# Two graph-attention layers with a mixture of experts: one pair a step and shared weight fetches in the tail, and the second layer's weights prepared later

## The chip, the cores and the metric

The kernel runs on one core of a Trainium2 chip. A core has five engines that run side by side, each with its own queue of instructions that it takes in order: PE (TensorE, matrix products), DVE (VectorE, elementwise work, sums and 32x32 transposes), ACT (ScalarE, functions of one argument), POOL (GpSimd, here small elementwise work and the indirect transfers) and SP (SyncE, which only issues transfers). PEld is the loading of PE's stationary operand. The metric is the time of one execution on the device, in microseconds. Before the change the median of three runs was 1665.73 us (1664.08 to 1666.54).

## The reference

The input x is 64 batches of 256 rows of 256 float32 numbers, with one 256 x 256 adjacency matrix for all batches. With LN for the layer norm, the reference does

```
x = x + elu(heads(softmax(mask(leaky_relu(e_src + e_dst))) @ q))   q = LN(x) @ W0, 4 heads of 64
x = x + LN(x) @ Wf.T + bf
x = x + relu(softmax(mask(leaky_relu(e_src + e_dst))) @ h)         h = LN(x) @ W1, one head
t = LN(x)
logits = t @ router.T ; the two largest of 8, weights renormalised to sum 1
x = x + t + sum over the two experts of weight * (gelu(t @ w1[e] + b1[e]) @ w2[e] + b2[e])
```

where e_src and e_dst are the products of q (or h) with the two halves of a vector a. The last layer is a mixture of 8 experts of which each row uses two.

## The kernel before

**The work.** A batch of 256 rows is two tiles of 128 rows. `batch_layers` carries a batch through both attention layers, the linear layer between them and the router's logits, in 20 pieces. Piece by piece it yields, so that the pieces of several batches interleave. The weights of an attention layer are widened by columns that yield e_src and e_dst directly: `score_columns` multiplies the weights with both halves of a (DVE, line 197), sums (200), scales, and subtracts the column mean (`center`, 158), which spares the norm's mean later. `prepare_f` transposes and centers the weights of the linear layer; `fill_mask` turns the adjacency into a mask, on PE through a transpose.

**The experts.** The first 62 batches are *routed*: 12 chunks of 4 batches, 6 of 2 and 2 of 1 (`CHUNKS`). When a chunk's logits are there, `route` places each row, twice, in a region of DRAM for its expert (`send`, line 877, an indirect transfer on POOL). As regions fill, `expert_pair` takes 256 rows of one expert (a *pair* of tiles): four transfers of 64 KB bring them into xr, one brings the row numbers and weights (xt), one brings the expert's 288 KB of first-layer weights (`we`, from the packed copy `wpack`). DVE turns the rows (sT, line 116), PE makes ph (`hidden`, 783), ACT applies gelu, PE makes py with the resident second-layer weights (`result`, 798), DVE adds b2 (y, 804), ACT scales by the row weights (776). Then `scatter` adds the 256 rows to the output with two indirect adding transfers on POOL (815). Each pair's adds wait until the adds of the pair before have landed (`added[-2:]`), because two pairs may hold the same row. The last pieces are 14 *flush* pairs, which hold what is left in the regions. There are 131 pairs in all.

The last two batches are *dense*: `dense_expert(b, e)` runs all 8 experts on all 256 rows of a batch and adds them to `base` with weights that are zero for the experts not chosen, so it needs no sends and no adds to DRAM.

**What sets the order.** From line 1041 the order of instructions is written out by hand, in *steps*. `active` holds the running generators, each with a rank; in a step every one advances by one yield, lowest rank first; a negative rank goes on within the step. A step number divided by 3 gives a phase. A batch begins every three steps (phase 2), the first in step 2, the last in step 191. `setup` jobs begin one a step from step 3 (`SETUP_AT`): prepare_f, prepare1 (the second attention layer's `score_columns`), the second mask, prepare_r, then `pack_expert` for each expert (which loads an expert's weights and writes the packed copy). In phase 1 pairs begin: two a time while batches are still to come, then three. In phase 2 up to two dense jobs begin. One scatter is issued a step. What the steps fix is the order in each engine's queue; an engine waits only where an operand, or a free buffer, is missing. `WBUFS`, `XBUFS` and `YBUFS` are the numbers of buffers for we, xr and y. `later` holds a routing job until a phase that it names.

Work issued ahead of line 1041 (constants, the first mask, the first layer's weights) is placed by the planner of the framework.

Of the kernel before, what the change touches and what calls it, by code (L numbers as in the profile page):

```python
# [9 lines left out]
F32 = mybir.dt.float32  # L10
# [17 lines left out]
def kernel(  # L28
# [108 lines left out]

    adj_i = work.tile([P, NT, N], adj.dtype, tag="z", name="adj_i", bufs=6)
    nc.scalar.dma_start(out=adj_i, in_=adj.rearrange("(t p) j -> p t j", p=P))

# [4 lines left out]
    def fill_mask(layer, op):  # L145
        mf = work.tile([P, NT, N], F32, tag="xT", name=f"maskf{layer}", bufs=4)
        nc.vector.tensor_scalar(mf, adj_i, 0.0, None, op0=op)
        pm = bank("pm", [NT, N])
        for t in range(NT):
            for j in range(NT):  # L150
                nc.tensor.transpose(
                    pm[:, j, t * P : (t + 1) * P], mf[:, t, j * P : (j + 1) * P], ident
                )
        nc.vector.tensor_copy(masks[layer], pm)

    fill_mask(0, ALU.is_gt)

# [9 lines left out]
    def gnn_weights(w, a, heads, slope, name):  # L167

        rows = lambda w, k: (
            w.rearrange("(p k) o -> k p o", k=KT) if heads > 1
            else w.rearrange("(k p) o -> k p o", k=KT)
        )[k]
        d = D // heads
        wx = const.tile([P, KT, heads, d + 3], F32, tag=name, name=name)  # L180
        for k in range(KT):
            nc.sync.dma_start(
                out=wx[:, k, :, :d],
                in_=rows(w, k).rearrange("p (h d) -> p h d", h=heads),
            )
        av = work.tile([P, 2, d], F32, tag="e", name=name + "_a", bufs=1)
        nc.scalar.dma_start(out=av.rearrange("p s d -> p (s d)"), in_=rows_to_all(a, 2 * d))
        flat = wx.rearrange("p k h c -> p k (h c)")
        return flat, lambda: score_columns(wx, av, heads, slope, name)

    def score_columns(wx, av, heads, slope, name):
        d = D // heads
        flat = wx.rearrange("p k h c -> p k (h c)")
        prod = work.tile([P, heads, d], F32, tag="hp", name=name + "_p", bufs=1)
        for k in range(KT):
            for s, c in ((0, d + 1), (1, d)):
                nc.vector.tensor_mul(
                    prod, wx[:, k, :, :d], av[:, s : s + 1, :].to_broadcast([P, heads, d])
                )
                nc.vector.tensor_reduce(wx[:, k, :, c : c + 1], prod, AX.X, ALU.add)  # L200
            nc.vector.tensor_scalar(
                wx[:, k, :, d + 1 : d + 2], wx[:, k, :, d + 1 : d + 2], 1.0 - slope, None,
                op0=ALU.mult,
            )
            nc.vector.tensor_scalar(
                wx[:, k, :, d + 2 : d + 3], wx[:, k, :, d : d + 1], slope - 1.0, None,
# [3 lines left out]

    wx0, prepare0 = gnn_weights(w0, a0, H, SLOPE0, "wx0")
    xblk = {0: load_blocks(0)}
    xin = {0: load_batch(0)}
    prepare0()
    wx1, prepare1 = gnn_weights(w1g, a1g, 1, SLOPE1, "wx1")

# [8 lines left out]
    def prepare_f():  # L225
        pw = bank("pw", [KT, D])
        for t in range(KT):
            for k in range(KT):
                nc.tensor.transpose(
                    pw[:, k, t * P : (t + 1) * P], wf_in[:, t, k * P : (k + 1) * P], ident  # L230
                )
        nc.vector.tensor_copy(wfT, pw)
        center(wfT, D)

        nc.vector.tensor_scalar(bias_f, bias_f, -1.0, None, op0=ALU.add)

    r_in = work.tile([E, D], F32, tag="x1b", name="r_in", bufs=1)
    nc.scalar.dma_start(out=r_in, in_=router)
# [10 lines left out]
    C_B1, WROW = KT * D, KT * D + 64  # L249
    WBUFS, XBUFS, YBUFS = 7, 5, 7  # L250
    wpack = tc.dram_tile([E, P, WROW], F32, name="wpack")
# [47 lines left out]
    def once(work):  # L299
# [6 lines left out]
        lambda work=work: once(work)  # L306
        for work in (prepare_f, prepare1, lambda: fill_mask(1, ALU.not_equal), prepare_r)
    ]
# [103 lines left out]
    def projected1(xT, rstd, b):  # L412
# [12 lines left out]
        for t, pq in enumerate(pqs):  # L425
# [3 lines left out]
            )  # L429
        me = work.tile([P, NT, N], F32, tag="me", name="me")  # L430
        for j in range(NT):
# [278 lines left out]
    def expert_pair(j, n, ids, ef, regs, needs):  # L710
# [23 lines left out]

        xt = small.tile([P, 2, ROW - D], F32, tag="xt", name="xt", bufs=12)
        loads.append(
# [17 lines left out]
        )  # L754
        yield 95
        xT = turned(work.tile([P, KT, PAIR], F32, tag="sT", name="sT", bufs=3), xr)
        w = small.tile([P, 2], F32, tag="w", name="w", bufs=8)
        yield 30
# [34 lines left out]

    def result(hT, e):
        py = bank("py", [2, D])
        for t in range(2):
            for f in range(KT):
# [3 lines left out]
                    start=(f == 0), stop=(f == KT - 1),  # L801
                )
        y = io.tile([P, 2, D], F32, tag="y", name="y", bufs=YBUFS)
        nc.vector.tensor_add(y, py, b2s[:, e, :].to_broadcast([P, 2, D]))  # L804
# [25 lines left out]

    def dense_expert(b, e):

        own = dense_batch[b]
        yield 90
        we = io.tile([P, WROW], F32, tag="we", name="we", bufs=WBUFS)
        nc.sync.dma_start(out=we, in_=wpack[e])
        yield 40
        yield 30
        hT = hidden(own["xT"], we)
        yield 80  # L840
        y = result(hT, slice(e, e + 1))
        for t in range(NT):
            nc.vector.scalar_tensor_tensor(
                own["base"][:, t, :], y[:, t, :], own["w"][:, t, e : e + 1],
                own["base"][:, t, :], op0=ALU.mult, op1=ALU.add,
            )
        if e == E - 1:
            while b == B - 1 and (scatters or len(added) < 2 * PAIRS):
                yield 99
            d = nc.sync.dma_start(  # L850
                out=out_rows[b * N : (b + 1) * N, :].rearrange("(t p) d -> p t d", p=P),
                in_=own["base"],
            )
            before = added[-2:] + based if b == B - 1 else []
            tc.declare_no_dep(
                d.ins, query=SYNC, group="out", keep=before,
                reason="no row is added to here, or every add is in their chain",
            )
            for ins in before:
                tc.add_manual_dep(d.ins, ins.name, AFTER, reason="filling rows were added here")  # L860
            tc.add_to_no_dep_group("out", d.ins)
            nc.sync.nop()

# [24 lines left out]
    def later(rank, *phases):  # L888

        yield rank  # L890
        while order_steps[-1] % TICKS not in phases:
            yield rank
# [103 lines left out]
    def route_dense(b, lg):  # L996
# [13 lines left out]
        dense_batch[b]["w"] = w  # L1010
        dense_jobs.extend(lambda e=e: dense_expert(b, e) for e in range(E))

# [3 lines left out]
    def jobs():  # L1016
        b = done = taken = 0
        for c, nb in enumerate(CHUNKS + (1,) * DENSE):
            nt = nb * NT
            lg = keep.tile([P, nt, E], F32, tag="lg", name=f"lg_{c}", bufs=10)  # L1020
            xng = []
# [17 lines left out]
    step, more, credit = 2, True, 0.0  # L1039
    SETUP_AT = 3  # L1040
    with tc.manual_schedule():
        while more or active or waiting or dense_jobs or scatters:
# [6 lines left out]
            if step >= SETUP_AT and setup:  # L1049
                begin(setup.pop(0)(), 90)  # L1050
            if phase == 1:
                credit = min(credit + (2.0 if more else 3.0), 3.0)
                while waiting and credit >= 1.0:
                    credit -= 1.0
                    begin(waiting.pop(0)(), 90)
            if phase == 2:
                for _ in range(2):
                    if dense_jobs:
                        begin(dense_jobs.pop(0)(), 90)
            if scatters:  # L1060
# [53 lines left out]
```

## Time and profile before

| what | value |
|---|---|
| median of the runs | 1665.73 us |
| the profiled execution's own time | 1670.08 us |
| its span, first to last instruction | 1668.3 us |
| busy: PE, DVE, ACT, POOL | 1495.5, 1317.4, 833.2, 889.4 us |
| mean granted PE clock | 0.958 |
| bytes moved | 209.74 MB, mean 126 GB/s |
| we fetches | 147 of 288 KB |
| indirect adds (line 815) | 262, 416.7 us of POOL |
| indirect sends (line 877) | 248, 251.1 us of POOL |

The span is what the engines show; the execution's own time has a little around it. Busy time is an average over stages that differ, so the stages have to be looked at one by one. A line such as "x started; idle 3.31 <- DMA out_dram" says that the engine stood idle for 3.31 us before this instruction, and that the last thing to arrive was that transfer. A transfer's issue on an engine's queue is not its duration: it lands later.

### The profile page before, as it was taken

Reading aid. Unit: us, or ns where it says so; the run is one execution under the profiler, and the core shown is the slowest. Engines: PE = TensorE matmul, PEld = TensorE weight load, DVE = VectorE, ACT = ScalarE, POOL = GpSimd, SP = SyncE. Lnnn points to the kernel's source line nnn. Section 1 sums busy time; section 2 is a strip of 40 time slices with the busy share of each in tenths; the row PEclk is TensorE's granted clock in tenths of the full one; section 3 lists DMA queues with packets and bytes.
Section 4 is the critical chain, followed back from the end, with each engine's and each line's share of the span. In section 5 each row is a group of like instructions: output and inputs, shape, how many; then the busy total and the mean of one; then the engine's idle time right before and its main releaser. Section 6 shows DMA issues by size and latency. Waiting matters only on the chain.

```text
span 1668.3 us, 30242 instructions
## 1 busy us (share of the span) xinstructions
PE 1495.5 (90%) x8474; PEld 1311.2 (79%) x8474; DVE 1317.4 (79%) x4478; ACT 833.2 (50%) x1832; POOL 889.4 (53%) x853
## 2 busy tenths in 40 slices
PE   5898888899999999999999999999989987678782
PEld 4777777688888888888888888888878876567671
DVE  6888989999898988898989898998889876423330
ACT  0243444455656666666666665655555565323221
POOL 0121433545757575757575757574764666444344
PEclk8999999999999999999999999999999998879986
DMA  3812223255757575756575766665564676866753
GB/s 107 231 41 58 61 70 94 74 142 114 167 118 163 118 159 129 140 132 146 133 149 134 145 133 146 137 140 121 123 142 99 115 156 141 200 135 112 155 107 44
DMA packets 365285, 209.74 MB, mean 126 GB/s; under 512 B 264376, under 2 KB 335040, under 8 KB 365120
## 3 DMA queue, kind: packets, MB, share of 16 engines
q1 hardware_dynamic: 314496, 139.43, 34.0%
q0 software_dynamic: 49632, 67.39, 22.5%
q8 instruction: 70, 1.15, 0.3%
q10 hardware_dynamic: 992, 0.99, 0.2%
q14 instruction: 95, 0.78, 0.2%
HBM read 118.55 MB, written 89.15 MB: 124 GB/s over the span
## 4 chain that ended last, share of the span: by engine, by line
PE 55%; DVE 26%; DMA 6%; issue 5%; POOL 4%; ACT 2%; SPq 1%; DVEq 0%; POOLq 0%; ACTq 0%
PE ph L783 14%; PE pv L475 12%; PE py L798 9%; PE pq L384 5%; PE pq L419 4%; DVE z L461 4%; PE pf L529 4%; DVE stats L353 4%; DMA out_dram<-y,xt 3%; PE pt L368 3%; POOL out_dram L815 2%; DVE mv L354 2%; PE pl L599 2%; PE pd L454 1%; DVE x L535 1%
## 5 line engine op out<-in xcount | busy, mean ns | idle before, releaser
L815 POOL DMA_INDIRECT out_dram<-y,xt x262 | 416.7, 1591 | 255.4 <-DMA out_dram<-y,xt 73.0
L475 PE MATMUL pv<-q,z 128*128 128x65 f32 (+1 forms) x2560 | 369.8, 299 | 6.7 <-DVE z L461 5.3
L475 PEld LDWEIGHTS pv<-q,z 128*128 128x128 f32 x2560 | 331.9, 194 | 19.5 <-DVE z L461 5.8
L783 PE MATMUL ph<-sT,we 128*128 128x256 f32 x1048 | 259.1, 405 | 56.2 <-DVE sT L116 47.1
L361 POOL TENSOR_SCALAR rstd<-mv 128x4 f32<-128x4 f32 (+1 forms) x132 | 69.7, 528 | 436.1 <-DVE mv L354 352.9
L877 POOL DMA_INDIRECT xs<-xng,pos x248 | 251.1, 1012 | 69.2 <-issue 66.9
L783 PEld LDWEIGHTS ph<-sT,we 128*128 128x128 f32 x1048 | 209.8, 205 | 90.9 <-DVE sT L116 50.6
L798 PE MATMUL py<-w2s,hT 128*128 (+1 forms) x1176 | 263.9, 379 | 1.4 <-DVE z L461 0.7
L798 PEld LDWEIGHTS py<-w2s,hT 128*128 128x128 f32 x1176 | 219.7, 190 | 29.7 <-DVE z L461 1.0
L374 ACT COPY xT<-pt 128x512 f32<-128x512 f32 x192 | 113.3, 590 | 222.4 <-PE pt L368 184.7
L804 DVE TENSOR_TENSOR y<-py,b2s 128x512 f32<-128x512 f32 x147 | 97.5, 688 | 158.9 <-PE py L798 88.7
L789 ACT ACTIVATE hT<-ph,we 128x256 f32<-128x256 f32 x294 | 122.8, 471 | 183.3 <-PE ph L783 80.9
L461 DVE SCALAR_TENSOR_TENSOR z<-pd,q,mask 128x256 f32<-128x256 f32 x512 | 211.1, 473 | 0.3 <-PE pd L454 0.2
L362 POOL TENSOR_TENSOR rstd<-rstd,mhalf 128x4 f32<-128x4 f32 (+1 forms) x132 | 162.6, 1232 | 11.0
L776 ACT ACTIVATE y<-y,w 128x256 f32<-128x256 f32 x262 | 113.1, 501 | 104.4 <-DVE y L804 96.3
L353 DVE BATCH_NORM_STATS2 stats<-x 128x6 f32<-128x256 f32 x384 | 156.3, 407 | 2.2
L384 PE MATMUL pq<-wx,xT 128*128 128x268 f32 x512 | 137.9, 415 | 8.6 <-DVE wt L257 4.2
L419 PE MATMUL pq<-wx,xT 128*128 128x259 f32 x512 | 129.1, 394 | 15.5 <-ACT xT L374 11.2
L529 PE MATMUL pf<-wfT,xT 128*128 128x256 f32 x512 | 125.0, 388 | 0.0
L419 PEld LDWEIGHTS pq<-wx,xT 128*128 128x128 f32 x512 | 91.9, 189 | 41.9 <-ACT xT L374 22.4
L384 PEld LDWEIGHTS pq<-wx,xT 128*128 128x128 f32 x512 | 100.9, 202 | 30.1 <-issue 6.9
L551 ACT ACTIVATE rel<-pv,rinv 128x256 f32<-128x256 f32 x128 | 54.0, 474 | 108.2 <-DVE rinv L482 95.8
(151 smaller groups left out, 2233.8 us busy)
## 6 DMA issues: line engine op xcount, KB each, us to landing
we<-wpack SPq DMA_DIRECT2D x147, 288.0 KB
xr<-xs SPq DMA_DIRECT2D x524, 64.0 KB
xblk<-in_x_dram SPq DMA_DIRECT2D x256, 64.0 KB
xin<-in_x_dram SPq DMA_DIRECT2D x64, 256.0 KB
out_dram<-base SPq DMA_DIRECT2D x64, 256.0 KB
out_dram<-y,xt POOLq DMA_INDIRECT x262
xs<-xng,pos POOLq DMA_INDIRECT x248
xs<-fill SPq DMA_DIRECT2D x9, 260.0 KB
```

The costliest lines, as they stand in the source:

```text
L353: nc.vector.bn_stats(stats[:, t, :], src[:, t, :])
L362: nc.gpsimd.tensor_tensor(rstd[:, :n], rstd[:, :n], mhalf[:, :n], ALU.pow)
L384: nc.tensor.matmul(pq.rearrange("p h c -> p (h c)"), xT[:, k, t * P : (t + 1) * P], wx[:, k, :], start=(k == 0), stop=(k == KT - 1),)
L419: nc.tensor.matmul(pq, xT[:, k, t * P : (t + 1) * P], wx1[:, k, :], start=(k == 0), stop=(k == KT - 1),)
L461: nc.vector.scalar_tensor_tensor(z[:, j, :], pd[:, i, :], q[:, j, h, d + 2 : d + 3], mask[:, j, :], op0=ALU.max, op1=ALU.mult,)
L475: nc.tensor.matmul(pv[:, h, :], z[:, j, t * P : (t + 1) * P], q[:, j, h, : d + 1], start=(j == 0), stop=(j == NT - 1),)
L529: nc.tensor.matmul(pf[:, t, :], xT[:, k, t * P : (t + 1) * P], wfT[:, k, :], start=(k == 0), stop=(k == KT - 1),)
L783: nc.tensor.matmul(ph[:, f, :], we[:, k * D + f * P : k * D + (f + 1) * P], xT[:, k, :], start=(k == 0), stop=(k == KT - 1),)
L789: nc.scalar.activation(hT[:, f, :], ph[:, f, :], AF.Gelu, bias=we[:, C_B1 + f : C_B1 + f + 1])
L798: nc.tensor.matmul(py[:, t, :], hT[:, f, t * P : (t + 1) * P], w2s[:, e, f * D : (f + 1) * D].rearrange("p e c -> p (e c)"), start=(f == 0 ...
L815: d = nc.gpsimd.indirect_dma_start(out=out_rows, out_offset=bass.IndirectOffsetOnAxis(ap=xt[:, t, 0:1].bitcast(I32), axis=0), in_=y[:, t, ...
L877: d = nc.gpsimd.indirect_dma_start(out=xs_d[: E * CAP * PAIR, :], out_offset=bass.IndirectOffsetOnAxis(ap=at, axis=0), in_=xe, in_offset=None,
```

## The change

**Start-up.** The adjacency goes to a buffer of another tag (xr instead of z), and its load is issued after that of a0. The first mask is made after the first layer's weights. Copies of the masks and of wfT out of PSUM go from DVE to ACT. `score_columns` makes both products into one tile and sums them at once; of its products those of the second half of the first layer's rows, and all of the second layer's, go to POOL. One Exp on a constant column is issued early. `setup` begins in step 4, with three empty steps after prepare_f, so that the second layer's weights, the second mask and the router come in steps 8 to 10 and the packing from step 11.

**Tail.** Three pairs begin per three steps from step 180 on (`DRAIN_AT`) instead of from the step in which the batches run out; from step 209 (`QUIET`) one pair begins in each step, unless three results are queued for adding. A dense job is now one expert for both dense batches: the weights are fetched once, the two batches follow one another, and the result is added to `base` straight from PSUM, then b2. One dense job begins every other step. The output of a dense batch is issued by a job of its own. When no batch is left, `later` no longer waits for a phase, and a pair's turned rows rank ahead of the results. Buffers: y 9 instead of 7, xt 14 instead of 12, w 12 instead of 8, me 1 instead of 2, lg 7 instead of 10.

```diff
-    adj_i = work.tile([P, NT, N], adj.dtype, tag="z", name="adj_i", bufs=6)
-    nc.scalar.dma_start(out=adj_i, in_=adj.rearrange("(t p) j -> p t j", p=P))
...
-        nc.vector.tensor_copy(masks[layer], pm)
-
-    fill_mask(0, ALU.is_gt)
+        nc.scalar.copy(masks[layer], pm)
...
-        prod = work.tile([P, heads, d], F32, tag="hp", name=name + "_p", bufs=1)
+        nc.vector.tensor_scalar(av[:, 0, :], av[:, 0, :], 1.0 - slope, None, op0=ALU.mult)
         for k in range(KT):
-            for s, c in ((0, d + 1), (1, d)):
-                nc.vector.tensor_mul(
-                    prod, wx[:, k, :, :d], av[:, s : s + 1, :].to_broadcast([P, heads, d])
-                )
-                nc.vector.tensor_reduce(wx[:, k, :, c : c + 1], prod, AX.X, ALU.add)
...
+            eng = nc.vector if heads > 1 and k == 0 else nc.gpsimd
...
+            for i, part in enumerate((1, 0)):
+                eng.tensor_tensor(
+                    prod[:, i], wx[:, k, :, :d],
+                    av[:, part : part + 1, :].to_broadcast([P, heads, d]), ALU.mult,
+                )
+            nc.vector.tensor_reduce(
+                wx[:, k, :, d : d + 2].rearrange("p h c -> p c h"), prod, AX.X, ALU.add
+            )
...
+    adj_i = io.tile([P, NT, N], adj.dtype, tag="xr", name="adj_i", bufs=5)
+    nc.scalar.dma_start(out=adj_i, in_=adj.rearrange("(t p) j -> p t j", p=P))
     xblk = {0: load_blocks(0)}
     xin = {0: load_batch(0)}
     prepare0()
+
+    warm = small.tile([P, 1], F32, tag="warm", name="warm", bufs=1)
+    nc.scalar.activation(warm, ones[:, :1], AF.Exp)
+    fill_mask(0, ALU.is_gt)
...
-        nc.vector.tensor_copy(wfT, pw)
+        nc.scalar.copy(wfT, pw)
...
-    WBUFS, XBUFS, YBUFS = 7, 5, 7
+    WBUFS, XBUFS, YBUFS = 7, 5, 9
...
-        for work in (prepare_f, prepare1, lambda: fill_mask(1, ALU.not_equal), prepare_r)
+        for work in (
+
+            prepare_f, *[lambda: None] * 3,
+            prepare1, lambda: fill_mask(1, ALU.not_equal), prepare_r,
+        )
...
-        yield 95
+
+        yield 95 if more else 75
...
-    def dense_expert(b, e):
-
-        own = dense_batch[b]
+    def dense_expert(e):
+
         yield 90
         we = io.tile([P, WROW], F32, tag="we", name="we", bufs=WBUFS)
         nc.sync.dma_start(out=we, in_=wpack[e])
         yield 40
-        yield 30
-        hT = hidden(own["xT"], we)
-        yield 80
-        y = result(hT, slice(e, e + 1))
...
+        for b in range(ROUTED, B):
+            own = dense_batch[b]
+            yield 35
+            hT = hidden(own["xT"], we)
+            yield -85
+            py = product(hT, slice(e, e + 1))
+            for t in range(NT):
+                for add in (py[:, t, :], b2s[:, e, :]):
+                    nc.vector.scalar_tensor_tensor(
+                        own["base"][:, t, :], add, own["w"][:, t, e : e + 1],
+                        own["base"][:, t, :], op0=ALU.mult, op1=ALU.add,
+                    )
+            if e == E - 1:
+                begin(store_dense(b), 99)
...
-        while order_steps[-1] % TICKS not in phases:
+        while more and order_steps[-1] % TICKS not in phases:
...
+    DRAIN_AT, QUIET = TICKS * (B - 4), TICKS * B + 17
+    SETUP_AT = 4
...
-            if phase == 1:
-                credit = min(credit + (2.0 if more else 3.0), 3.0)
+            if step >= QUIET:
+                if waiting and len(scatters) < 3:
+                    begin(waiting.pop(0)(), 90)
+            elif phase == 1:
+                credit = min(credit + (2.0 if step < DRAIN_AT else 3.0), 3.0)
                 while waiting and credit >= 1.0:
                     credit -= 1.0
                     begin(waiting.pop(0)(), 90)
-            if phase == 2:
-                for _ in range(2):
-                    if dense_jobs:
-                        begin(dense_jobs.pop(0)(), 90)
+            if dense_jobs and step % DENSE == 0:
+                begin(dense_jobs.pop(0)(), 90)
```

`product` is the matrix part of the old `result`, split off; `store_dense` is the output part of the old `dense_expert`.

## The prediction

> **What bounds the kernel now.** I read the busy tenths first, then a table of busy time by stage, then the adds on POOL in order of time, then the chain, the waits of the last 320 us, and last the start-up in order of time. In the table the columns are the stretch, its length, busy time (and instructions) of PE, PEld, DVE, ACT and POOL, the granted clock, the DMA share and GB/s.
>
> ```profile
> 1272.00:1296.00 24.00, 23.76 (x142) 21.22 (x141) 22.62 (x86) 14.73 (x31) 13.24 (x12) 1.00 0.49 97
> ...
> 1363.00:1388.00 25.00, 18.38 (x81) 15.54 (x80) 17.61 (x88) 10.30 (x22) 15.32 (x15) 0.86 0.78 153
> ...
> 1460.00:1490.00 30.00, 20.37 (x80) 17.12 (x80) 8.35 (x20) 6.92 (x16) 14.12 (x10) 0.78 0.63 113
> ...
> 1623.00:1668.00 45.00, 12.31 (x48) 10.21 (x48) 4.59 (x12) 5.24 (x12) 18.52 (x12) 0.66 0.35 44
> ```
>
> Until about 1340 us PE and DVE are full. From 1363 no engine is; POOL is busiest beside its load elsewhere, and its order of time says why:
>
> ```profile
> 1379.23 1.61 POOL L815 DMA_INDIRECT out_dram<-y,xt  x1 [0.30 <-issue]
> 1381.15 1.58 POOL L815 DMA_INDIRECT out_dram<-y,xt  x1 [0.31 <-ACT xng L569]
> 1382.17 0.74 POOL L578 IOTA xng<- 128x2 int32 x1
> 1386.22 1.56 POOL L815 DMA_INDIRECT out_dram<-y,xt  x1 [3.31 <-DMA out_dram<-y,xt]
> ```
>
> The two adds of a pair leave together; the next pair's wait for both to land. At the very end, with everything else done, the chain is this loop alone:
>
> ```profile
> 1645.54 1.54 POOL out_dram L815
> 1647.09 0.30 issue
> 1647.39 3.67 DMA out_dram<-y,xt
> 1651.19 0.71 issue
> 1651.90 1.54 POOL out_dram L815
> ```
>
> A pair thus costs at least 6.4 us (1651.90 less 1645.54). From 1429.50 to the last at 1658.29 there are 33 pairs, 32 spacings, 7.15 us each: the tail is a row of adds near its floor. PE's stalls there are a consequence:
>
> ```profile
> PE ph L783 <- DVE sT L116: 47.1, 10, 9.8
> ...
> DVE y L804 <- DMA out_dram<-y,xt: 28.1, 8, 6.2
> ```
>
> Three pairs begin together; DVE can't write a result until an add has freed one of 7 y buffers; the next turned rows sT stand behind it on DVE, and PE behind those. The start-up holds the other part:
>
> ```profile
> 15.71 3.78 PE L384 MATMUL pq<-wx,xT 128*128 128x268 f32 x8
> ...
> 17.78 1.28 ACT L392 ACT_TABLE_LOAD   x1 [17.78 <-PE pq L384]
> ...
> 20.23 0.42 DVE L197 TENSOR_TENSOR wx_p<-wx,wx_a 128x256 f32<-128x256 f32 x1
> ...
> 26.27 1.66 DVE L461 SCALAR_TENSOR_TENSOR z<-pd,q,mask 128x256 f32<-128x256 f32 x4
> ```
>
> The first projection has its inputs at 12.6 (wx0 centered, same view) but starts at 15.71, behind the transposes and the mean of wf; a table load follows; then the second layer's columns keep DVE from the first scores z.
>
> **What the Trainium skill says.** "DMA: Bandwidth & Descriptors", Rules for kernel authors: beside another access of the same bytes, an accumulating DMA must wait for the earlier one's semaphore. So the row of adds can't be overlapped by the new order; the gap of 3.0 to 3.8 us between pairs agrees. "TensorE: Matmul & The Clock Gate", What's actually happening: after an idle window of about 3.4 us PE falls to half clock. The trace agrees: 24 ph matmuls took 8.28 us after 9.83 us idle, 5.45 after 3.02. "ScalarE: Activation LUTs", What ACT_TABLE_LOAD costs: 1283 ns for a load; the trace has 1.28 us. "GPSIMD Engine Reference", 3.1: a two-input float32 product of 2048 elements takes 4497 ns on POOL, so I estimate 0.56 us for 256; no row of before shows one (DVE's takes 0.42).
>
> **The change, part by part.** Sums are against the profiled execution: span 1668.3, its time 1670.1; the median of the runs, 1665.7, is 2.6 below the span, and I carry the difference over.
>
> *Start-up.* prepare_f goes behind the projection: 15.71 less 12.6, -3.1. The warm Exp hides the table load: -1.3. So the scaled q of batch 0 comes some 4.5 earlier. wf's PE work (1.06 + 2.07 with a copy between, now 0.6 on ACT) then stands before the first pd, but DVE no longer spends 20.23 to 26.17 on the second layer (8 products and sums at 0.42, four small ones, two centering subtractions 0.76): z starts about 20.5, -5.8. The second mask (0.38 + 0.69 and PE's 1.09 between) also leaves step 5: -8 by step 6. It all returns in steps 8 to 10, less what moved to POOL and ACT: two sums over twice 256 (0.75 each, by the 128x512 rows at 0.69), small ones 0.5, centering 0.76, 0.38, 0.14: 3.3 on DVE, plus PE 1.2 + 1.1 + 0.4. Four products on POOL are 2.2, and DVE, in order, can wait for the last about 1 us, with the turned xT and the stats of other batches queued behind it; DVE has idle spots there (1.6 at 36.2, 1.7 at 46.8) that hide about 1. Net -4; bounds -8 (all hidden) and +2 (products at 1.5 us each). On the queues: adj now goes behind a0 on ACT's, so a0 (awaited 1.3) is earlier; mask 0 needs adj only in step 5. The packing's DMAs on SP and its 0.11 us memsets on DVE move four steps later; the first pair's ph comes at 286 us, so no one waits. Work outside the hand-written order may be placed otherwise; that lies in the bounds.
>
> *Buffers at no cost.* me with one buffer: written in one step, read in the next, rewritten three steps later. lg with 7: a slot's old reader is 19 steps gone when it is written; if the cover failed, DVE's 0.14 us copy would wait. xt, w, y get more.
>
> *Tail, by the loop's steps.* I worked the rules through step by step. Before: 2 to 241; after: 2 to 238. Credit 3 begins at step 180 instead of 194, so at steps 184, 187, 190 and 193 one pair more begins. By step 210 the adds of pair (15,2) leave instead of (14,2): four pairs earlier. One unit of expert work is 8 ph and 8 py: 40 took 8.90 and 40 took 8.55 in the chain (1512.79 and 1521.69), so (8.90 + 8.55)/5 = 3.49 us of PE.
> - Four pairs pulled into steps 184 to 209: 4 x 3.49 = 14 on PE, 4 x (0.63 sT + 0.69 y + 0.4 w) = 7 on DVE. PE is full up to 1343, then 18 of 25: +12 taken; bounds +5 and +30 (POOL full, below).
> - Four fewer pairs in the row behind step 210: 4 x 7.15 = -28.6.
> - From step 209 a step begins one pair, and every other step one dense weight block, used by both batches in turn: 8 fetches of 288 KB fewer. PE per step is 2 x 3.49 = 7.0, just under the row's 7.15, without the 10 us holes, so at full clock; DVE per step is 0.63 + 0.4 + 0.69 + four updates of 0.44 (two more, less the 0.69 add) = 3.5; SP per step 1.9 + 0.4 + 0.5 + 0.25. All hide under 7.1; without that cover each would cost its excess 20 times. The gate of fewer than 3 queued results skips a pair at step 212, and step 222 has no add: +5 (0 if PE runs ahead, 7 if not).
> - Fewer, evenly spread transfers: spacing can fall from 7.15 to 6.9 or so in about 20 steps: -4; bounds 0 and -15 (floor 6.4).
> - Sends and logits are no longer held to phases once no batch is left, the fill comes at step 207 instead of 209, the dense output is issued as a job of its own: all beside the row, 0.
>
> The stall goes where? No longer y buffers (9, and at most a few queued): next late is the add's landing, then PE. Sum: -4 + 12 - 28.6 + 5 - 4 = -19.6. Span 1648.7, runs 1646.
>
> **Rivals.**
> (1) *The adds of steps 188 to 209 run as slowly as those among sends now.* From 1369.19 to 1429.50 seven spacings took 8.62 each, with two to four sends (1.0 each) and norms between. 22 steps at 8.62 are 190 from 1268.3 (first add of the chunk, 1272.3 less 4), so 1458; 27 spacings at 7.15 and the hole give 1658, and 10 after it: span 1668, runs 1662 to 1666. For it: POOL's gaps there hold sends already. Against: its 13.2 of 24 busy at 1272.
> (2) *The row at its floor*: start-up -8, extra +6, then 27 x 6.6 = 178 from 1436.7 - 2 instead of 221.6: span 1623, runs 1620. For it: the last nine spacings average 6.58. Against: PE's 7.0.
> (3) *Slower.* POOL is in order; an add in nearly every full step puts its 3.0 to 3.8 us wait in front of rstd (L361), and the projections' exp and all behind wait for rstd. If 11 of those 22 steps take the whole 3.3, that is +36: span 1685, runs 1682. It decides from 0.9 us a step on (19.6/22). Before has POOL wait for DVE (353 us on mv), which speaks against; two pairs per three steps never tried it at three.
> (4) *It doesn't do what it says*: if SP, in order, holds single fetches behind we buffers, PE stays starved. By the steps a we slot is freed 1.7 steps before it is asked for and used three after, so I leave this inside (1).
>
> **How the numbers follow.** Main 0.56 (runs 1636 to 1656), (1) with (4) 0.18, (2) 0.10, (3) and a worse start-up 0.16. Within 0.2% (3.3 us) is about what a measurement can't tell from no change: 0.05, out of (1). Faster 0.56 + 0.10 + 0.13 = 0.79, slower 0.16. The range 1624 to 1664 leaves out (3), 0.16, and the lower part of (2), some 0.04.
>
> **What would show it.** Right: first z near 20 us; no 10 us PE holes after 1440; the last add's start near 1639, spacings near 7; the first add of the last four-batch chunk 3 to 5 earlier. Wrong: POOL's rstd waiting behind adds in 1250 to 1440; spacing above 8 after step 210; DVE waiting for POOL's products for several us at step 8.

## The result and the profile after

The changed kernel takes 1652.48 us (median of 4 runs, 1651.71 to 1656.37) against 1665.3 for the kernel before, measured beside it: a ratio of 0.9926, with a 95% interval of 0.9914 to 0.9938. The profiled execution has a span of 1650.1 us (own time 1651.89). The span fell by 18.2 and the medians by 12.8. Most of the difference is that the profiled execution of before (1670.08) lay 4.8 above its own median.

The busy time by stage (columns as in the prediction), with the stretches shown before and two others, after:

```profile
1272.00:1296.00 24.00, 23.76 (x140) 21.26 (x139) 21.91 (x77) 14.02 (x33) 12.34 (x12) 1.00 0.58 117
1363.00:1388.00 25.00, 22.06 (x106) 18.63 (x106) 19.05 (x102) 12.92 (x29) 17.32 (x16) 1.00 0.72 149
1460.00:1490.00 30.00, 29.39 (x137) 25.53 (x136) 13.22 (x28) 10.94 (x27) 12.81 (x9) 1.00 0.80 165
1500.00:1550.00 50.00, 50.00 (x234) 44.01 (x233) 24.84 (x56) 18.80 (x44) 19.38 (x13) 1.00 0.74 144
1605.00:1650.00 45.00, 0.00 (x0) 0.00 (x0) 0.00 (x0) 0.00 (x0) 18.51 (x12) 0.50 0.35 44
```

From 1460 to 1490 PE is busy for 29.4 of 30 us, where it was 20.4 at a clock of 0.78. In the last 45 us no engine but POOL works. Its order of time there, after:

```profile
1626.86 1.54 POOL L833 DMA_INDIRECT out_dram<-y,xt  x1 [2.98 <-DMA out_dram<-y,xt]
1628.71 1.54 POOL L833 DMA_INDIRECT out_dram<-y,xt  x1 [0.30 <-issue]
1633.31 1.54 POOL L833 DMA_INDIRECT out_dram<-y,xt  x1 [3.06 <-DMA out_dram<-y,xt]
1635.16 1.54 POOL L833 DMA_INDIRECT out_dram<-y,xt  x1 [0.30 <-issue]
1639.74 1.54 POOL L833 DMA_INDIRECT out_dram<-y,xt  x1 [3.04 <-DMA out_dram<-y,xt]
```

Two adds, a wait of 3 us for both to land, two adds: 6.4 us a pair. The last pair starts at 1639.74 (before: 1658.29). The waits from 1430 us on (engine, line, what it waited for: total, times, longest), after:

```profile
POOL out_dram L833 <- DMA out_dram<-y,xt: 47.4, 15, 4.3
...
PE ph L797 <- DMA we<-wpack: 11.3, 1, 11.3
DVE sT L116 <- DMA xr<-xs: 9.0, 3, 3.6
DVE y L822 <- DMA out_dram<-y,xt: 4.4, 1, 4.4
```

PE's waits for turned rows (sT) are gone. From 1430 us on before had 39.6 us of them in 8 waits. One wait of PE for a weight block, of 11.3 us, is left; it ends at 1444.99. The start-up in order of time, after:

```profile
11.23 3.94 PE L397 MATMUL pq<-wx,xT 128*128 128x268 f32 x8 [0.53 <-DVE wx L161]
...
19.75 1.65 DVE L474 SCALAR_TENSOR_TENSOR z<-pd,q,mask 128x256 f32<-128x256 f32 x4
...
36.03 2.09 PE L159 MATMUL pc<-wx,mean_w 128*128 128x259 f32 x4 [7.86 <-DVE wx L208]
...
43.26 1.09 PE L149 MATMUL pm<-ident,maskf 128*128 128x128 f32 x4 [3.43 <-DVE maskf L145]
...
44.14 3.78 PE L397 MATMUL pq<-wx,xT 128*128 128x268 f32 x8
```

The first projection starts 4.5 us earlier and the first z 6.5 earlier. But when the second layer's weights come, PE stands idle for 7.9 us, then for 3.4, and makes the next projection cold, that is, at half clock (3.78 us; at full clock, at 22.17, it takes 2.04). The first pair's add is at 319.2, against 318.2 before: by then all is given back.

To place the gain I number the pairs as they are added and use the starts of their first adds. A runs from pair 82 (first of the last four-batch chunk) to pair 104, which the prediction calls (15,2); B from there to pair 118, the first flush pair; C to the last pair. A *spacing* is the time from one pair's first add to the next pair's. All in us, from one profiled execution each; the ratios are those on record, and the quotients of the medians differ from them by up to 0.0025 (most in e5, 0.9892):

| kernel | ratio to before (95%) | pair 1 | pair 82 | A | B | C | last |
|---|---|---|---|---|---|---|---|
| before | 1 | 318.2 | 1272.3 | 194.2 | 103.2 | 88.6 | 1658.3 |
| after | 0.9926 (0.9914 to 0.9938) | 319.2 | 1269.6 | 183.8 | 103.2 | 83.2 | 1639.7 |
| e1 | 0.9903 (0.9885 to 0.9921) | 320.1 | 1269.1 | 179.4 | 102.5 | 83.2 | 1634.2 |
| e2 | 0.9960 (0.9943 to 0.9976) | 319.7 | 1270.5 | 196.4 | 100.2 | 84.6 | 1651.7 |
| e3 | 0.9908 (0.9887 to 0.9929) | 319.3 | 1269.8 | 181.2 | 105.7 | 83.9 | 1640.6 |
| e4 | 0.9910 (0.9881 to 0.9940) | 321.3 | 1272.0 | 181.8 | 103.0 | 85.7 | 1642.5 |
| e5 | 0.9867 (0.9828 to 0.9906) | 317.4 | 1268.1 | 182.6 | 104.1 | 83.4 | 1638.2 |
| e6 | 0.9923 (0.9897 to 0.9949) | 318.1 | 1268.9 | 182.4 | 106.7 | 83.7 | 1641.8 |
| e7 | 0.9904 (0.9872 to 0.9937) | 318.4 | 1267.2 | 183.0 | 105.8 | 83.3 | 1639.3 |
| e8 | 0.9897 (0.9866 to 0.9928) | 320.5 | 1271.0 | 182.3 | 104.5 | 84.7 | 1642.6 |
| e9 | 0.9949 (0.9934 to 0.9965) | 318.6 | 1275.4 | 184.3 | 100.9 | 91.1 | 1651.7 |
| e10 | 0.9821 (0.9796 to 0.9846) | 316.9 | 1271.8 | 183.0 | B + C 173.5 | | 1628.3 |
| e11 | 0.9847 (0.982 to 0.9874) | 318.3 | 1276.0 | 178.1 | 94.6 | 83.8 | 1632.5 |
| e12 | 0.9792 (0.9767 to 0.9817) | 312.9 | 1271.2 | 184.8 | B + C 172.6 | | 1628.6 |

How finely this can be read: after, e7, e8 and e11 are the same up to step 208, and their A still spreads from 178 to 184. A difference of 5 us in A between two profiles says nothing by itself. B lies between 100.2 and 106.7 in all rows that give it but that of e11. The median of before on the chips used lies between 1665 and 1674, so kernels are compared by their ratios.

**How long a result waits for its add.** I counted results (two scalings of y on ACT for each pair) and adds in order. The last three results of before, and then the last of after:

```profile
1633.15 0.91 ACT L776 ACTIVATE y<-y,w 128x256 f32<-128x256 f32 x2 [1.56 <-DVE y L804]
1634.94 0.91 ACT L776 ACTIVATE y<-y,w 128x256 f32<-128x256 f32 x2 [0.88 <-DVE y L804]
1636.66 0.91 ACT L776 ACTIVATE y<-y,w 128x256 f32<-128x256 f32 x2 [0.82 <-DVE y L804]
```

```profile
1588.61 0.91 ACT L790 ACTIVATE y<-y,w 128x256 f32<-128x256 f32 x2 [4.16 <-DVE y L822]
```

The last result of before is complete at 1637.57, and its add starts at 1658.29. From pair 100 on every result lies ready before its add, by 9.7 to 38 us in before and by 22 to 50 us in after. So behind pair 104, where POOL does nothing but adds, neither PE nor ACT holds an add, not even in before with its holes on PE. What a pair costs there is the two issues (1.54 each, 0.3 between) and the wait for the adds of the pair before to land. In B this wait has a mean of 4.0 us in both kernels; in C it is 3.4 in before and 3.0 in after. C by stage, before and then after:

```profile
1570.00:1658.00 88.00, 57.82 (x243) 48.72 (x241) 25.63 (x57) 21.79 (x50) 39.89 (x26) 0.84 0.53 84
```

```profile
1556.50:1640.00 83.50, 27.95 (x130) 24.26 (x128) 13.85 (x32) 13.13 (x30) 40.36 (x27) 0.68 0.38 48
```

Between 1570 and 1620 before still fetches 8 weight blocks and 22 blocks of rows (64 KB each); from 1556 on after fetches one weight block and no rows.

### The profile page after: what moved, and what is told of

Its sections match the earlier page's. It is cut to its first block, busy times and chain, and to the rows that moved or that the text cites. A ratio compares the mean times of both kernels' runs of the same rounds, so it can differ in the third digit from the quotient of the medians.

```text
span 1650.1 us, 30208 instructions
## 1 busy us (share of the span) xinstructions
PE 1476.0 (89%) x8474; PEld 1299.7 (79%) x8474; DVE 1319.7 (80%) x4479; ACT 832.7 (50%) x1836; POOL 891.5 (54%) x859
## 4 chain that ended last, share of the span: by engine, by line
PE 61%; DVE 22%; DMA 5%; POOL 5%; issue 3%; ACT 3%; SPq 1%; POOLq 0%; DVEq 0%; ACTq 0%
PE pv L488 14%; PE ph L797 13%; PE py L812 12%; PE pq L397 5%; PE pq L432 5%; PE pf L542 4%; DVE z L474 4%; DVE stats L366 3%; PE pt L381 3%; DMA out_dram<-y,xt 3%; POOL out_dram L833 3%; PE pl L612 2%; DVE mv L367 2%; ACT xT L387 1%; PE pd L467 1%
## 5 line engine op out<-in xcount | busy, mean ns | idle before, releaser
L797 PE MATMUL ph<-sT,we 128*128 128x256 f32 x1048 | 244.9, 387 | 13.5 <-DMA we<-wpack 11.3
L797 PEld LDWEIGHTS ph<-sT,we 128*128 128x128 f32 x1048 | 200.4, 195 | 40.8 <-issue 11.7
L822 DVE TENSOR_TENSOR y<-py,b2s 128x512 f32<-128x512 f32 x131 | 85.7, 686 | 64.9 <-PE py L812 50.7
```

Source lines behind the costliest of these rows:

```text
L797: nc.tensor.matmul(ph[:, f, :], we[:, k * D + f * P : k * D + (f + 1) * P], xT[:, k, :], start=(k == 0), stop=(k == KT - 1),)
```

## The experiments

**e1: the tail without the start-up.** The kernel before with all edits of the tail; masks, `score_columns`, warm Exp and setup order stay.

```diff
-    WBUFS, XBUFS, YBUFS = 7, 5, 7
+    WBUFS, XBUFS, YBUFS = 7, 5, 9
...
+    DRAIN_AT, QUIET = TICKS * (B - 4), TICKS * B + 17
```

> The start-up of before with the tail of after. Theory (the second layer's preparation in step 8 gives back all that the start-up gained, 1.0 us more than that in the trace): as fast as after or up to 1 us faster, 1651 to 1654. Rival (the start-up is worth the predicted 4 us and something later swallowed it in the trace): 1655 to 1658. In the trace the row-number fill of batch 0 comes at 93.4 us as in before, 94.4 in after.

Measured 0.9903, about as fast as the whole change (0.9926; the intervals overlap). The start-up part contributes nothing that can be measured.

**e2: without the earlier third pair.**

```diff
-                credit = min(credit + (2.0 if step < DRAIN_AT else 3.0), 3.0)
+                credit = min(credit + (2.0 if more else 3.0), 3.0)
```

> After, with two pairs per three steps until the batches have run out, as before; one pair a step from step 209 and the shared fetches stay. By the steps the last adds come at step 242 instead of 238. Theory (four pairs fewer stand in the row of adds behind step 210, and that is the gain): 10 to 16 us are lost, 1662 to 1668, no better than before. Rival (the gain is the steady PE and the shared fetches): at most 4 us are lost, 1652 to 1657.

Measured 0.9960: about half of the gain goes, 5.7 us by the ratios, which is less than the theory's 10 and more than the rival's 4. A is back at 196.4 (before 194.2), B + C stay shorter than before's (184.8 against 191.8).

**e9: the earlier third pair alone**, in the kernel before.

```diff
-                credit = min(credit + (2.0 if more else 3.0), 3.0)
+                credit = min(credit + (2.0 if step < TICKS * (B - 4) else 3.0), 3.0)
```

> The kernel before with one edit: the third pair of a round begins from step 180 instead of 194; three pairs in one step, two dense jobs for two fetches and all buffers stay as they were. Theory (the gain is the four pairs that leave the row of adds at the end): the add of step 210 is that of pair (15,2) and comes within 5 us of the 1453 of the changed kernel, and the time is some 10 less than before, 1653 to 1659. Rival (the earlier pairs pay only together with the one-a-step order and the shared fetches): without these the last 27 pairs keep a spacing of 7.15 or more with holes on PE, and the time is 1660 to 1668.

Measured 0.9949, which is 8.5 us of 1665. Pair 104's add is at 1459.7, 6.3 after the changed kernel's, so the 5 us of the theory were missed; but pair 82 came 5.8 later in this execution and A is the same (184.3). C stays long (91.1); PE is still busy for 27 of the 40 us from 1600 on. Together e9 (-0.51%) and e2 (-0.40%) make -0.91%, which is the whole gain within the intervals: as far as these tell, two parts of about equal size that add.

**e3 and e4: which of the tail's other edits?** e3 lets three pairs begin together also after step 209; e4 gives each dense batch its own fetch of the weights.

```diff
-            if step >= QUIET:
-                if waiting and len(scatters) < 3:
-                    begin(waiting.pop(0)(), 90)
-            elif phase == 1:
+            if phase == 1:
```

> After, with three pairs every third step to the end instead of one a step from 209. By the steps the last adds come at 237 instead of 238. Theory (the row of adds sets the end, and PE has slack behind it once the pairs are ahead): within 4 us of after, 1650 to 1657. Rival (pairs that begin together starve PE and then the row, as in before): the holes of before return, 1659 to 1666.

> After, with the weights fetched once for each dense batch, as before: 8 fetches of 288 KB more. Theory (transfers are hidden beside the row of adds; they only lengthen some landings): 0 to 3 us slower, 1652 to 1656. Rival (the fetches held the row or PE): 6 or more us slower.

0.9908 and 0.9910: neither the one pair a step nor the shared fetch is needed for the gain, though the change's description names both. Each was left out alone; leaving out both was not run.

**e7: is PE the limit in B?** In the waits and the chain of the changed kernel PE carries B. The chain that ended last there (start, duration, work), after:

```profile
1510.20 3.45 PE ph L797 x16
1513.65 3.45 PE py L812 x16
1517.11 3.45 PE ph L797 x16
1520.56 3.45 PE py L812 x16
```

This is 6.9 us a step, and PE is busy 50.00 of 50 us. So I took half of ph away, about a quarter of PE's work; the output then lacks it.

```diff
-            for k in range(KT):
+            used = 1 if order_steps[-1] >= QUIET else KT
+            for k in range(used):
...
-                    start=(k == 0), stop=(k == KT - 1),
+                    start=(k == 0), stop=(k == used - 1),
```

> After, leaving out half of the first product (k = 1 of ph) of every expert unit from step 209 on, some 36 units at 0.9 us of PE each. Theory (PE bounds the stretch from the adds of (15,2) to the first flush pair, 103 us for 14 spacings, and the row of adds bounds what follows): that stretch shrinks to 92 to 97 us, the last 13 spacings stay at 83, the whole 6 to 11 us faster than after. Rival A (the row bounds all of it): no change. Rival B (PE bounds all): 25 us or more faster.

Busy time by stage, e7:

```profile
1500.00:1550.00 50.00, 38.13 (x168) 31.21 (x168) 23.91 (x56) 16.20 (x42) 21.29 (x15) 1.00 0.67 127
```

PE falls to 38 of 50, B stays (105.8), the ratio stays (0.9904). My theory fell: a PE that is full, and that the chain runs through, was not what set the end. The adds were. The results now lie ready up to 59 us before their adds, which start no earlier.

**e11: then why is a pair 7.4 us in B and 6.4 in C?** The waits of the adds in B are longer, and the profile names something else at their end. POOL in order of time, after:

```profile
1511.32 1.54 POOL L833 DMA_INDIRECT out_dram<-y,xt  x1 [4.07 <-DMA xt<-xs]
1513.17 1.54 POOL L833 DMA_INDIRECT out_dram<-y,xt  x1 [0.30 <-ACT hT L803]
1518.00 1.57 POOL L833 DMA_INDIRECT out_dram<-y,xt  x1 [3.29 <-DMA out_dram<-y,xt]
1519.87 1.54 POOL L833 DMA_INDIRECT out_dram<-y,xt  x1 [0.30 <-ACT hT L803]
1525.53 1.54 POOL L833 DMA_INDIRECT out_dram<-y,xt  x1 [4.12 <-DMA xt<-xs]
```

No add reads hT, and an add's own result and xt are there long before: such a name is only that of what ended last. The waits are 3.1 to 5.4 us in B, with a mean of 4.0, where they are 2.9 to 3.1 in C; the DMA share is 0.77 in B against 0.38 in C. e11 takes the fetches of weights away.

```diff
+        if order_steps[-1] >= QUIET and kept and kept[1] < 4:
+            we = kept[0]
+            kept[1] += 1
+        else:
+            we = io.tile([P, WROW], F32, tag="we", name="we", bufs=WBUFS)
...
```

> The changed kernel, but from step 209 on only every fourth pair fetches an expert's first-layer weights; the pairs between and the dense jobs use the block that is there already (so they compute with another expert's weights: what is left out is the right block, all arithmetic, adds and other transfers stay). About 28 of 35 fetches of 288 KB go. Theory (from 1453 to 1557 the spacing is 7.4 instead of 6.4 because the adds land later beside the fetches): the stretch from pair (15,2) to the first flush pair falls from 103 to 90 to 96 us. Rival (the spacing there comes from something else on POOL or in the order of steps, transfers do not matter): 101 to 106 us.

Busy time by stage, and then POOL in order of time, e11:

```profile
1500.00:1550.00 50.00, 50.00 (x234) 44.01 (x233) 25.03 (x57) 18.61 (x44) 22.88 (x15) 1.00 0.62 91
```

```profile
1501.73 1.54 POOL L839 DMA_INDIRECT out_dram<-y,xt  x1 [3.08 <-DMA out_dram<-y,xt]
1503.58 1.54 POOL L839 DMA_INDIRECT out_dram<-y,xt  x1 [0.30 <-issue]
1508.15 1.54 POOL L839 DMA_INDIRECT out_dram<-y,xt  x1 [3.03 <-DMA xr<-xs]
1510.00 1.54 POOL L839 DMA_INDIRECT out_dram<-y,xt  x1 [0.30 <-ACT y L795]
1514.87 1.54 POOL L839 DMA_INDIRECT out_dram<-y,xt  x1 [3.33 <-ACT hT L808]
```

B falls by 8.6 to 94.6, with the mean wait at 3.4 (3.0 to 4.5) and PE as full as in the changed kernel. So the adds land later beside the fetches. B of the changed kernel has 24 fetches of weights and e11's has 4: 8.6 us for 20 is 0.43 each. By this estimate the 8 fetches that the change saves are worth 3.4 us at most, too little for e4 to show.

**e6: do norms wait behind adds?** e6 puts a step's rstd on POOL ahead of sends and adds.

```diff
+                if entry[0] >= 94 and half_done:
+                    finish_norms(NT)
                 entry[0] = next(entry[2], None)
```

> After, with the rest of a step's norms put on POOL ahead of that step's sends and adds instead of behind them. Theory (between 1270 and 1450 the batches wait for rstd behind sends and waiting adds, which is why the four pairs pulled forward cost more than 12 us): the stretch from the first add of the last four-batch chunk to that of pair (15,2), 183.8 us in after, shrinks to 172 to 178, the whole to 1643 to 1650. Rival (PE's own work fills that stretch): within 3 us of after.

The waits from 1268 to 1460, after and then e6:

```profile
DVE by L573 <- POOL rstd L375: 16.0, 3, 8.1
```

```profile
DVE by L573 <- POOL rstd L375: 7.1, 4, 5.4
```

The wait is there and e6 more than halves it, yet A is 182.4, where the theory had 172 to 178, and the ratio is 0.9923. The delay of a norm there is not on the way to the end.

**e8: dense jobs spread over three steps instead of two.**

```diff
-            if dense_jobs and step % DENSE == 0:
+            if dense_jobs and step % 3 == 0:
```

> After, with a dense job every third step instead of every second, so that PE has 5.8 us of expert work a step where the row of adds needs 6.4. The dense work ends in step 238 instead of 230. Theory (PE bounds the stretch with two units a step while it idles 66 us at the end): the stretch from (15,2) to the first flush pair shrinks from 103 to 93 to 97 us, the last 13 spacings rise from 83 to 84 to 88, the whole 4 to 10 us faster than after. Rival (the row is the bound throughout): no change, or slower where the last dense work sets the end.

0.9897, B 104.5, C 84.7: B is no shorter, so this theory fell with that of e7, and the interval overlaps the changed kernel's. From 1450 to 1560 it fetches 27 weight blocks where the changed kernel fetches 25, so it doesn't test what the number of fetches does.

**e5: the second layer's weights in parts.** `score_columns` and `fill_mask` become generators that yield between products, sums, centering and mask, so that PE gets other work between.

```diff
+        if heads == 1:
+            yield 90
+            for k, prod in enumerate(prods):
+                sums(prod, k)
...
-        for work in (
-
-            prepare_f, *[lambda: None] * 3,
-            prepare1, lambda: fill_mask(1, ALU.not_equal), prepare_r,
+    setup += [prepare1, lambda: mask_parts(1, ALU.not_equal), lambda: once(none), lambda: once(prepare_r)]
```

> After, with the second layer's preparation cut into four steps (products in 7, sums in 8, mean on PE in 9, subtraction in 10) and the second mask into three (8, 9, 10), so that no PE product of the setup is queued before DVE has made its input. The work is the same. Theory (the start-up's gain was lost because PE, in order, stood idle 8 us behind the mean, and went cold): the row-number fill of batch 0 comes at 86 to 90 us instead of 94.4, and the whole is 4 to 8 us faster than after, 1645 to 1650. Rival (DVE's work itself gave it back): 93 us or later, as fast as after.

Measured 0.9867; the interval lies below the changed kernel's, but not below those of e1, e3, e4, e6, e7 and e8, which don't have this edit. The row-number fill comes at 92.5 us, where the theory had 86 to 90, and the first pair's add is only 1.8 us earlier than in the changed kernel. Its start-up by stage, e5:

```profile
22.00:28.00 6.00, 6.00 (x28) 5.60 (x26) 2.56 (x9) 0.43 (x2) 1.63 (x3) 0.53 0.37 86
28.00:34.00 6.00, 4.77 (x23) 4.40 (x24) 3.27 (x7) 0.63 (x1) 2.31 (x3) 0.50 0.01 1
34.00:40.00 6.00, 2.68 (x9) 1.82 (x8) 6.00 (x16) 0.58 (x1) 0.88 (x1) 0.50 0.27 55
```

In this execution PE ran at half clock from 22 to 40 us (the 32 products pv at 24 us took 6.93, in the changed kernel 3.68), which can hide what the split won. e12, with the same start-up, shows it without that.

**e10: a third dense batch**, so two pairs fewer in the row (7 us of PE less) for 8 units of expert work (28 us of PE more).

```diff
-    CHUNKS = (4,) * 12 + (2,) * 6 + (1, 1)
+    CHUNKS = (4,) * 12 + (2,) * 6 + (1,)
...
-    WBUFS, XBUFS, YBUFS = 7, 5, 9
+    WBUFS, XBUFS, YBUFS = 7, 5, 7
...
-            if dense_jobs and step % DENSE == 0:
+            if dense_jobs and step % 3 == 0:
```

> The changed kernel with a third dense batch in place of the last routed one: two pairs fewer to add (129), 8 units of expert work more for PE that need no add, one dense job in three steps instead of two, 7 y buffers instead of 9. Theory (the row of adds is what sets the time from 1450 on, PE has room): two spacings of 6.4 to 7.4 go, the time falls by 10 to 15 to 1637 to 1643. Rival (PE, which is 50 of 50 us busy between 1500 and 1550, is just as near): 8 units of 3.49 us are 28 us of PE less 7 for the two pairs, of which much comes before the pure row of adds; the time is between 1648 and 1662.

0.9821: B + C is 173.5 for 25 spacings, 12.9 less than 186.4 for 27, that is, two spacings of 6.4. By the ratios it is 17 us faster than the changed kernel, somewhat more than the theory's 10 to 15; what lies beyond the row is about as large as the intervals leave open. Busy time by stage, e10:

```profile
1550.00:1600.00 50.00, 48.81 (x225) 42.32 (x224) 23.27 (x52) 17.45 (x41) 24.16 (x16) 1.00 0.43 59
1595.00:1638.00 43.00, 16.68 (x72) 12.99 (x71) 9.31 (x20) 3.46 (x9) 18.69 (x12) 0.78 0.38 55
```

PE works until 1614, through 30 us in which it stood idle in the changed kernel, and the end doesn't notice. This is the row of adds as the bound, shown from the other side.

**e12: e5 and e10 together.**

> The changed kernel with the second layer's weights prepared in parts (e5) and the third dense batch (e10) together: the first is 300 us into the kernel and shortens the way to the first pair, the second is in the last 190 us and shortens the row of adds. Theory (the two are separate stretches, so their gains add): a ratio to the kernel before of 0.974 to 0.982, which is 1622 to 1636 on a before of 1665.7; the last stretch from pair (15,2) to the end is 172 to 175 us as in e10. Rival (a few us gained early are lost again before the tail, because the steps in between are paced by PE and DVE and the executions of one kernel already differ by 5 us there): 0.981 to 0.985, no better than e10.

0.9792 (medians 1640.34 us against 1673.71 on its chip): faster than the kernel before and than the changed one. The ratio is in the theory's range, but that it beats e10 is not shown, since the intervals overlap. Its start-up by stage, e12:

```profile
22.00:28.00 6.00, 5.68 (x43) 5.43 (x44) 3.77 (x13) 0.43 (x2) 1.64 (x3) 1.00 0.33 87
28.00:34.00 6.00, 1.49 (x11) 0.93 (x9) 5.86 (x13) 1.22 (x2) 3.19 (x3) 0.77 0.01 1
```

With PE at full clock at 22 the first add is at 312.9, 6.3 earlier than in the changed kernel and 4.0 earlier than in e10. At pair 82 the lead over e10 is 0.6 us, at pair 104 it is -1.3: in these two profiles what the start-up gains has faded before the tail, as the rival had it.

## Why the prediction was right, and where it was not

The sign and the row of adds as the bound were right. That the total came so near was in part luck: the predicted span was 1648.7 and the measured one 1650.1, but two errors of 8 and 9 us cancelled in it, and the profiled execution of before was long by itself. In the medians the gain is 12.8 us where 19.6 was forecast, two thirds. The parts of the sum, measured on the two profiles:

| step of the prediction | predicted | measured | how measured |
|---|---|---|---|
| start-up | -4 | -2.7 at pair 82, none of it from the start-up | pair 1 at +1.0; e1, without it, has pair 82 at 1269.1 too |
| four pairs pulled ahead | +12 | +19.4 | 82 to 104 now 183.8; 82 to (14,2) before, 1436.7 less 1272.3, 164.4 |
| four fewer in the row | -28.6 | -29.8 | before, 1436.7 to 1466.5 |
| hole and pacing, fewer transfers | +5 - 4 | -5.5 | 186.37 less 191.82 behind pair 104 |
| sum | -19.6 | -18.6 | |

- **Start-up.** The step "what returned in steps 8 to 10" failed. I counted 3.3 us of DVE and 2.7 of PE and about 1 of waiting. DVE's wait for the products was 1.3, but PE, in order, stood idle for 7.9 and 3.4 us behind the new columns and the mask and then ran cold. Each early term was right (z at 19.75, predicted 20.5). The products on POOL took 0.64 to 0.73 us each, not the estimated 0.56; the quoted 4497 ns is that of an addition. The -2.7 at pair 82 more likely belongs to the execution of before: it took 78.7 us from pair 73 to pair 80, where after, and e1 to e8, took 75.0 to 75.5 (e9 to e12, on other chips, 79.5 to 82.0).
- **Four pairs pulled ahead.** Right that they come cheaper than in the row; but +12 - 28.6 is a gain of 16.6, and alone this brings 8.5 us (e9), without it 5.7 of the gain are lost (e2). Under-sized was the price of the four: 4.9 us each, not 3. I took PE as the only cost, and PE was not it. Of the 50 us from 1400 PE is busy 31.3, at a clock of 0.77, and waits 11.3 us for weights whose fetch stands on SP behind the fill and three sets of rows; yet every result of A lay ready 16 to 38 us before its add. The adds stand in POOL's own order between sends and norms: POOL is busy for 116.7 of A's 183.8 us, and the mean spacing is 8.35. This is near to what rival (1) said, with 8.62 and pair 104 at 1458; the sum had it at 1444.7 (1436.7 - 4 + 12), and it came at 1453.4.
- **The row.** "PE per step is 7.0, just under the row's 7.15" was measured rightly (6.9) and named the wrong second limit. Spacing is 7.4 in B and 6.4 in C. e7 shows that PE doesn't set the 7.4, e11 that the fetches make up more than half of what it has above 6.4. In C the row is at rival (2)'s floor: PE ends at 1584.45, 55 us before the last add. My 3.0 to 3.8 us for the wait in before was its lower part: behind pair 104 it goes from 3.0 to 5.6. My +5 for a hole wasn't there: the longest spacing behind pair 104 is 8.8.
- **Cover.** I gave the one pair a step and the shared fetches as what ends the 10 us holes. The holes went (after 1445), but e3 and e4 show that neither alone is needed, and the holes themselves held no add: in before, too, the results lay ready. What the row gains is in C, 5.4 us for 13 waits whose mean fell by 0.4, where the fetches now end earlier: this is the term "fewer, evenly spread transfers" (-4), read from the traces of C and tested, in B, by e11. Which edit lets the fetches end earlier, and so gives the second half of the gain (e2), I did not separate. What remains are turned rows ranked ahead of results, dense results that take no y buffer, more y buffers and routing without phases. e10 and e12 have 7 y buffers and no wait of PE for turned rows, so 9 are not needed there. In e2 DVE waits 35.4 us for y buffers and PE not at all for turned rows; in e9, without the other edits, it is 16.1 and 36.2. That speaks for the rank; it is argued, not shown.
- **Rival (3)** has its mechanism in the trace (rstd held 8.1 us), but e6 shows it without effect. (4) shows as one wait of 11.3 us.
- **The carry-over.** Taking the median 2.6 below the span put the forecast at 1646; the median is 2.4 above the changed kernel's span. It held for one execution of before, which was long by itself, and makes most of the 6.5 us by which the median missed 1646.

So the row was 8 us cheaper than I had it and what lies ahead of it 9 dearer, and these cancelled. The main case was right in what bounds the end and in the direction of its two main tail terms, not in their sizes.

## What to carry to other kernels

When a row of dependent transfers ends a kernel, move members of the row to where other engines are full (e9: four pairs, 8.5 us), or replace them by work that needs no such transfer, even at several times the cost on an engine that already looks full (e10: 21 us more of PE for 13 less in the row). A full engine on the chain that ended last is a suspect, not a proof: look how long its results lie ready before they are used, and take a part of its work away and see. And price preparation work not only by its instructions but by how long the engine behind it stands still (here 7.9 and 3.4 us), and ask whether the gain lasts (in e12 it had faded before the tail).

## What was not expected of the hardware

- An indirect add's landing depends on what else is in flight. After the changed kernel's adds the mean wait was 3.0 us at a DMA share of 0.38 (C) and 4.0 at 0.77 (B); with most weight fetches gone it was 3.4 at 0.65 (B of e11).
- PE fell to half clock without a gap of 3 us just before. The Trainium skill, "TensorE: Matmul & The Clock Gate", Why this matters for your kernels, asks for no idle gaps above some 3 us between bursts. Us by us, after (columns as above):

```profile
1225.00:1226.00 1.00, 0.11 (x2) 0.00 (x0) 0.86 (x7) 1.00 (x3) 0.00 (x0) 1.00 0.90 105
1226.00:1227.00 1.00, 0.48 (x3) 0.38 (x3) 1.00 (x4) 1.00 (x3) 0.00 (x0) 1.00 0.18 26
1227.00:1228.00 1.00, 1.00 (x7) 0.81 (x7) 0.98 (x3) 0.19 (x1) 0.00 (x0) 1.00 0.00 0
...
1229.00:1230.00 1.00, 1.00 (x7) 1.00 (x6) 0.90 (x5) 0.00 (x0) 0.13 (x1) 0.50 0.71 144
...
1234.00:1235.00 1.00, 1.00 (x4) 0.70 (x3) 1.00 (x4) 0.24 (x1) 1.00 (x1) 0.50 1.16 176
```

A gap of 1.41 us ends at 1226.52, and some 2 us later, with PE busy again, comes half clock for 6.8 us. A gap of 3.05 us had ended 9 us before that, at 1219.89. In e9 two gaps of 0.47 and 0.51 us around one matmul (at 1160) were followed by the same 6.8 us, with no gap above 1 us in the 25 us before them; other gaps of 0.9 us had no such effect (before, at 1183). And in before the 24 ph matmuls at 1600.61 took 8.45 us after 3.18 us idle, less than the 3.4 that the prediction quotes. The measurement decides: in e9 the rule of 3 us wasn't enough to stay at full clock. That the short gaps are the cause is read from the order in time, not tested. Whether this explains why identical code differs by some 5 us between executions was not tested.
